# One PSUM bank moved from C's rows of a state-space scan to a third accumulator of the experts and attention

## The chip, the cores and the metric

The kernel runs on one core of one Trainium2 chip. The metric is the device time of one launch in microseconds; a verdict compares runs of two kernels on the same chip. Five engines work side by side, each on its own queue in order: TensorE (PE, with its weight loads shown as PEld), VectorE (DVE), ScalarE (ACT), GpSimd (POOL) and SyncE (SP), which issues nearly all DMAs.

## The reference, cut to what matters

Eight rows of x, 512 tokens by 256 channels each, go through two layers. Layer 0: a gate with eight exponential averages, a Mamba block, then a small expert-chosen linear map and a top-2 of 8 expert FFN. Layer 1: a linear pair with low-rank corrections, attention with 8 heads, an adapter with layernorm, and a top-4 of 32 expert FFN with a shared expert. All is float32. The change sits in the Mamba block:

```python
def step(h, inp):                                   # per token t
    x_t, dlt, B_t, C_t = inp                        # 512 channels, 16 states
    dA = jnp.exp(dlt[:, None, :] * A[None])
    h = dA * h + dlt[:, None, :] * B_t[:, :, None] * x_t[:, None, :]
    y_t = jnp.einsum('bn,bnd->bd', C_t, h) + D * x_t
    return (h, y_t)
...
y = ys.transpose(1, 0, 2) * jax.nn.silu(z)
return jnp.einsum('bld,md->blm', y, W_out)          # added to x
```

## The kernel before

The program is written as generators that yield after each piece of work, and a planner interleaves them; a compiler then fixes the order of each engine's queue. `thread_x` makes layer 0's gate and Mamba block, row by row. `thread_y` makes the rest for a group of rows: routing, experts' tiles, then attention. The groups are rows [0], [1, 2], [3, 4, 5], [6, 7]. While `thread_y` works on one group, `thread_x` is advanced so that the share of its cost that is done keeps step with the share of `thread_y`'s (L1170 to L1182). Row 0 of `thread_x` has no partner. The last group of `thread_y` runs beside the routing of layer 1's experts (`top4`), row 7's routing follows alone (L1201), then come 95 expert tiles and the final gather.

In `thread_x` a row has a head and 64 items. The head (`head`, L471 to L707) is cut into some 65 pieces: gate, averages, projections, convolution, and delta and delta times x, which go to DRAM as `packs`. It uses `gx`, a PSUM tag of two banks. Item n = (b, j, g, k) handles a quarter k of channel block j, 32 channels, with four of the 16 states, group g; so 128 partitions hold 32 channels by 4 states. `begin(n)` (L747) starts an item two ahead: ACT's exp gives dA (L752), POOL multiplies delta times x by B's row (L754, tile h, 8 buffers). `run(n)` (L774) lets DVE scan over time (L780) and multiply the result by C's row (L781). Four products later `add` (L785) lets PE sum them over the states into the bank `yp` (L790). `gate` and `finish` (L797, L805) complete the row: y times silu(z) on POOL, W_out on PE, the sum with x, and the store to `xa`.

The rows of B and C over 128 partitions come from a matmul of a 0/1 matrix (`states`) with the row's bf16 pieces. B's row is made once per (b, g), in a `gx` bank, and copied to SBUF by ACT (`get_B4`, L728). C's row is made by PE at k = 0 of every (b, j, g), 128 times in all, straight into a PSUM bank of its own, `c4` (L777 to L779), and DVE reads it there. The bank is single, so the next C matmul waits in PE's queue until the last product has read it. The chains written by `in_order` (L156) keep `thread_x`'s own instructions in program order on each engine.

PSUM has eight banks: gx 2, c4, yp in `thread_x`'s pool; g 2 and acc 2 in `thread_y`'s. `acc` (L870) takes the experts' transposed tokens and outputs, and attention's values, transposes and sums (L1032, L1062, L1078). In `top4`, the shared expert's two output banks are `yp` and `c4` (L1145).

Each item of the main loop also advances the head of a later row by one piece, and by a second at every twelfth (L852 to L854): some 70 pieces in a row's 64 items, so heads move ahead of their row over time.

Of the kernel before, what the change touches and what calls it, by code (L numbers as in the profile page):

```python
# [13 lines left out]
ALU = mybir.AluOpType  # L14
# [37 lines left out]
def adaln_attn_ffn_kernel(ctx: ExitStack, tc: tile.TileContext, d: dict, out: bass.AP):  # L52
# [23 lines left out]
    def mm(o, pairs):  # L76
        for i, (lhsT, rhs) in enumerate(pairs):
            nc.tensor.matmul(o, lhsT, rhs, start=(i == 0), stop=(i == len(pairs) - 1))  # L78
# [317 lines left out]
    def thread_x(wp, wk, ps):  # L396
        def load(name, shape):
            t = wp.tile(shape, F32, tag=name, name=name)
            nc.sync.dma_start(t, d[name])
            return t  # L400

        def gx():
            return ps.tile([P, T], F32, tag="gx", name="gx", bufs=2)
# [15 lines left out]
        W_in = load("W_in", [P, KC, 1024])  # L419
        W_x = load("W_x", [P, 4, 96])  # L420
        W_dt = load("W_dt", [64, 512])
        W_out = load("W_out", [P, 4, C])


        alpha = wp.tile([P, 9], F32, tag="alpha", name="alpha")
# [45 lines left out]
        def head(b):  # L471
# [97 lines left out]
            yield  # L569
            nc.gpsimd.tensor_tensor(soma[:, 1, :], soma[:, 1, :], s1, ALU.mult)  # L570
            yield
            cen = wk.tile([P, KC, T], F32, tag="cen", name="cen")
            sq = wk.tile([P, KC, T], F32, tag="gated", name="sq")
            p0 = project(Wout, soma, 0)
            yield
# [138 lines left out]
        def states(g):  # L714
            return quads[:, g].rearrange("k n c -> k (n c)")

        packs = [dram.tile([4, P, 2, T], F32, name=f"pack{i}", tag=f"pack{i}") for i in range(2)]
        xzs = [dram.tile([P, 4, 2, T], F32, name=f"xzs{i}", tag=f"xzs{i}") for i in range(2)]
        got, B4s = {}, {}

        def get_pack(b, j, k):

# [2 lines left out]
            nc.sync.dma_start(t, src[None].to_broadcast([4, 32, 2, T]))  # L725
            got[b, j, k] = t

        def get_B4(b, g):  # L728

            pt = gx()  # L730
            mm(pt, [(states(g), rows[b])])
            t = wk.tile([P, T], F32, tag="B4", name="B4", bufs=4)
            nc.scalar.copy(t, pt)
            B4s[b, g] = t


        fold = wp.tile([P, 32], F32, tag="fold", name="fold")
# [4 lines left out]
        ready = set()  # L742
        due, product = {}, []
        items = [(b, j, g, k) for b in range(NB) for j in range(4) for g in range(4) for k in range(4)]
        yps, Cs, hs, dAs, xz, y8s = {}, {}, {}, {}, {}, {}

        def begin(n):  # L747

            b, j, g, k = items[n]
            t = got[b, j, k]  # L750
            dA = wk.tile([P, T], F32, tag="dA", name="dA", bufs=4)
            nc.scalar.activation(dA, t[:, 0, :], AF.Exp, scale=A[:, 4 * j + k, g : g + 1])  # L752
            h = wk.tile([P, T], F32, tag="h", name="h", bufs=8)
            nc.gpsimd.tensor_tensor(h, t[:, 1, :], B4s[b, g], ALU.mult)  # L754
            hs[n], dAs[n] = h, dA
            if (g, k) == (1, 3):
                xz[b, j] = wk.tile([P, 2, T], F32, tag="xz", name="xz")
                nc.sync.dma_start(xz[b, j], xzs[b % 2][:, j])
            if j == 0 and g < 3 and k == 1:
                get_B4(b, g + 1)  # L760

            if j < 3 and (g, k) == (2, 3):
                get_pack(b, j + 1, 0)
            if j < 3 and g == 3 and k < 3:
                get_pack(b, j + 1, k + 1)
            if j == 3 and b + 1 < NB and g == 3:
                if k == 0:
                    get_pack(b + 1, 0, 0)
                if k < 3:
                    get_pack(b + 1, 0, k + 1)  # L770
                if k == 3:
                    get_B4(b + 1, 0)

        def run(n):  # L774
            b, j, g, k = items[n]
            h = hs[n]
            if k == 0:  # L777
                Cs[0] = ps.tile([P, T], F32, tag="c4", name="c4")
                mm(Cs[0], [(states(4 + g), rows[b])])  # L779
            nc.vector.tensor_tensor_scan(h, dAs.pop(n), h, 0.0, ALU.mult, ALU.add)  # L780
            product[:] = [nc.vector.tensor_tensor(h, h, Cs[0], ALU.mult).ins]  # L781
            if k == 3:
                due.setdefault(n + 1, []).append(lambda: add(n - 3))

# [12 lines left out]
        def gate(b, j, n):  # L797
# [4 lines left out]
            if j == 3:  # L802
                due.setdefault(n + 2, []).append(lambda: finish(b, 0, n + 2))

        def finish(b, e, n, x=None):  # L805

            if e == 0:
                x = wk.tile([P, KC, T], F32, tag="cen", name="xr")
                nc.sync.dma_start(x, d["x"][b])
            pt = gx()  # L810
            mm(pt, [(W_out[:, j, ts(e, P)], y8s[b][:, j, :]) for j in range(4)])

            def sum_():
                nc.vector.tensor_tensor(x[:, e, :], x[:, e, :], pt, ALU.add)
                if e == 0:
                    finish(b, 1, n + 1, x)
                else:
                    nc.sync.dma_start(xa[b], x)
                    done.add(b)

            due.setdefault(n + 1, []).append(sum_)

        def pieces():

            for b in range(NB):
                for i, _ in enumerate(head(b)):
                    if b == 0 and i == 14:
                        prepare()
                    yield

        H = pieces()
# [2 lines left out]
            yield 3  # L834
        for k in range(4):
            get_pack(0, 0, k)
        get_B4(0, 0)
        begin(0)
        begin(1)
        N = len(items)  # L840
        for n in range(N):
            b, i = divmod(n, 64)
            if i == 58 and b + 1 < NB:
                while b + 1 not in ready:
                    next(H)
                    yield 0
            if n + 2 < N:
                begin(n + 2)
            run(n)
            for f in due.pop(n, ()):  # L850
                f()
            next(H, None)  # L852
            if i % 12 == 4:
                next(H, None)  # L854
            yield 4
        while due:
            n = min(due)
            for f in due.pop(n):
                f()
            yield 4  # L860

    def thread_y(q, bs, ps):
# [5 lines left out]
            return ps.tile([P, T], F32, tag="g", name="g", bufs=2)  # L868

        def acc():  # L870
            return ps.tile([P, T], F32, tag="acc", name="acc", bufs=2)

        with ExitStack() as ph:
            wp = ph.enter_context(tc.tile_pool(name=f"w2_{q}", bufs=1))
# [214 lines left out]
    def top4(wp, wk, ps):  # L1089
# [7 lines left out]
        def ps_tile():  # L1097
            return ps.tile([P, T], F32, tag="gx", name="g4", bufs=2)
# [3 lines left out]
        def route(b):  # L1102
# [39 lines left out]
            yield from dispatch(b, c, ti, dest4, counts, wk, ps_tile, ps_tile, E4, K4, CAP4, tab4, "tab4")  # L1142

            yield 1
            yp = [ps.tile([P, T], F32, tag=t, name="y4p") for t in ("yp", "c4")]  # L1145
            for f in range(KC):
                pa = ps_tile()
                mm(pa, [(sh["Ws1"][:, k, ts(f, P)], c[:, k, :]) for k in range(KC)])
# [212 lines left out]
```

## Time and profile before

| | us |
|---|---|
| median of 3 runs | 4148.91 (4148.35 to 4155.98) |
| the profiled execution | 4169.97 |
| its span | 4168.2 |
| PE busy in it | 3258.9 (78%) |
| DVE busy | 2635.8 (63%) |
| ACT busy | 1799.2 (43%) |
| POOL busy | 1612.5 (39%) |
| mean granted TensorE clock | 0.875 of full speed |

Busy time is an average over stages. Row 0's scans run from 155 to 420 us, rows 1 to 5's from 420 to 2014, rows 6 and 7's to 2832; attention of the last group and the layer 1 routing run to 3740, the expert tiles to 4080, the gather to the end. A group of instructions is told by line, engine, operation, tile written and tiles read, shape and count; then busy time in us and the mean of one in ns; then the idle time of the engine just before them and what ended most of it. A row of the waits gives who waited for whom, us in total, times, and the longest.

### The profile page before, as it was taken

To read this page: it belongs to the slowest core of one execution; us is meant where nothing else is said; L and a number is where in the kernel's file an instruction comes from. 1 tells how busy PE (TensorE), PEld (TensorE's weight loads), DVE (VectorE), ACT (ScalarE), POOL (GpSimd) and SP (SyncE) were. 2 spreads that over 40 slices of the span, in tenths; PEclk is the share of its full clock that TensorE was granted. 3 is DMA by queue.
4 is the path that set the end of the run, shared out by engine and by line. 5 is a ranking of instruction groups with operands and counts; after the bars stand their busy time and mean duration, and the time that the engine had idled before them with its cause. 6 is when DMAs were issued, how large, how long until landed. Compare 5 with 4: busy or idle time off the path is not lost. (4 is left out here: it accounts for less than half of the span.)

```text
span 4168.2 us, 36840 instructions
## 1 busy us (share of the span) xinstructions
PE 3258.9 (78%) x10964; PEld 1653.5 (40%) x10964; DVE 2635.8 (63%) x4178; ACT 1799.2 (43%) x2890; POOL 1612.5 (39%) x1222
## 2 busy tenths in 40 slices
PE   4425586888577788798669698889988999969894
PEld 1101153333254333333337433333466444437772
DVE  4597886798966888888972555764432443433336
ACT  2425465457267367357345333442322343322222
POOL 0445645355536435336353421320043111134552
PEclk7656687998788899799889799999989999989996
DMA  4555676445345312312245312213044112118776
GB/s 107 204 182 205 216 280 217 152 176 206 129 162 163 95 49 84 97 58 74 83 147 187 125 51 72 63 53 100 23 177 146 56 49 75 36 59 260 244 237 223
DMA packets 159372, 554.77 MB, mean 133 GB/s; under 512 B 27731, under 2 KB 34290, under 8 KB 146757
## 3 DMA queue, kind: packets, MB, share of 16 engines
q1 hardware_dynamic: 135076, 501.35, 36.3%
q0 software_dynamic: 24096, 51.08, 3.3%
q8 instruction: 87, 1.43, 0.1%
q14 instruction: 113, 0.92, 0.1%
HBM read 453.00 MB, written 234.82 MB: 165 GB/s over the span
## 5 line engine op out<-in xcount | busy, mean ns | idle before, releaser
L754 POOL TENSOR_TENSOR h<-packed,B 128x512 f32<-128x512 f32 x512 | 813.0, 1610 | 895.4 <-PE yp L790 536.6
L780 DVE TENSOR_TENSOR_SCAN h<-dA,h 128x512 f32<-128x512 f32 x512 | 791.8, 1546 | 77.1 <-POOL h L754 55.6
L752 ACT ACTIVATE dA<-packed,Aexp 128x512 f32<-128x512 f32 x512 | 357.7, 717 | 497.6 <-DVE h L780 346.3
L174 POOL DMA_INDIRECT tok<-ys,to_i x310 | 313.6, 1012 | 456.1 <-DVE ys L959 222.3
L1082 PE MATMUL acc<-aT,V 128*128 128x512 f32 x1024 | 454.3, 598 | 4.1 <-DVE aT L1066 3.9
L781 DVE TENSOR_TENSOR h<-h,c 128x512 f32<-128x512 f32 x512 | 350.1, 684 | 81.5 <-PE c L78 67.5
L174 POOL DMA_INDIRECT tab<-row,si x192 | 198.3, 1033 | 511.3 <-issue 235.4
L1082 PEld LDWEIGHTS acc<-aT,V 128*128 128x128 f32 x1024 | 193.5, 191 | 248.6 <-issue 231.6
L78 PE MATMUL acc<-wv,c 128*128 128x512 f32 x512 | 262.3, 630 | 4.7 <-DVE aT L1066 3.1
L1052 DVE TENSOR_REDUCE nm<-g 128x1 f32<-128x512 f32 x256 | 164.4, 682 | 115.9 <-PE g L1042 114.4
L78 PE MATMUL g<-xT,fw 128*128 128x256 f32 x960 | 231.2, 394 | 7.8 <-ACT h L952 7.8
L78 PE MATMUL acc<-fw,h 128*128 128x256 f32 x960 | 223.1, 386 | 5.2 <-DVE ys L959 5.2
L78 PE MATMUL c<-bc,quads 96*128 96x512 bf16 x128 | 57.8, 451 | 209.0 <-DVE h L781 205.5
L790 PE MATMUL yp<-h,fold 128*32 128x512 f32 x1024 | 217.5, 742 | 0.7 <-DVE h L781 0.7
L1055 ACT ACTIVATE ex<-g,nm 128x512 f32<-128x512 f32 x256 | 173.6, 683 | 102.8 <-DVE nm L1052 98.2
L78 PEld LDWEIGHTS g<-xT,fw 128*128 128x128 f32 x960 | 186.7, 199 | 44.7 <-ACT h L952 9.4
L78 PEld LDWEIGHTS acc<-fw,h 128*128 128x128 f32 x960 | 184.7, 194 | 44.9 <-issue 8.3
L1065 PE MATMUL acc<-ident,ex 128*128 128x128 f32 x1024 | 154.1, 283 | 53.6 <-ACT ex L1057 17.1
L1057 ACT ACTIVATE ex<-ex,den 128x512 f32<-128x512 f32 x256 | 176.6, 720 | 35.3 <-DVE den L1056 34.5
L1086 DVE TENSOR_TENSOR x<-x,acc 128x512 f32<-128x512 f32 x64 | 43.6, 682 | 231.2 <-PE acc L1082 231.2
L1065 PEld LDWEIGHTS acc<-ident,ex 128*128 128x128 f32 x1024 | 118.9, 143 | 176.3 <-issue 51.5
L1042 PE MATMUL g<-qk 64*128 64x512 f32 x512 | 159.8, 671 | 33.2 <-ACT ex L1055 20.6
(284 smaller groups left out, 5720.4 us busy)
## 6 DMA issues: line engine op xcount, KB each, us to landing
fw<-in_fW SPq DMA_DIRECT2D x60, 1154.0 KB
tab<-zeros SPq DMA_DIRECT2D x32, 2112.0 KB
packed<-pack SPq DMA_DIRECT2D x128, 512.0 KB
mw<-in_mW SPq DMA_DIRECT2D x95, 384.0 KB
tab<-zeros SPq DMA_DIRECT2D x16, 2080.0 KB
xt<-tab SPq DMA_DIRECT2D x95, 264.0 KB
pack<-dd SPq DMA_DIRECT2D x32, 512.0 KB
xz<-xzs SPq DMA_DIRECT2D x32, 512.0 KB
```

The lines of the kernel that those rows point to most:

```text
L78: nc.tensor.matmul(o, lhsT, rhs, start=(i == 0), stop=(i == len(pairs) - 1))
L174: i = nc.gpsimd.indirect_dma_start(out=table_, out_offset=bass.IndirectOffsetOnAxis(ap=idx, axis=0), in_=src, in_offset=None, bounds_check ...
L752: nc.scalar.activation(dA, t[:, 0, :], AF.Exp, scale=A[:, 4 * j + k, g : g + 1])
L754: nc.gpsimd.tensor_tensor(h, t[:, 1, :], B4s[b, g], ALU.mult)
L780: nc.vector.tensor_tensor_scan(h, dAs.pop(n), h, 0.0, ALU.mult, ALU.add)
L781: product[:] = [nc.vector.tensor_tensor(h, h, Cs[0], ALU.mult).ins]
L790: chain([nc.tensor.matmul(yps[0][32 * k : 32 * k + 32, :], fold, hs.pop(n + k), start=(g == 0), stop=(g == 3)) for k in range(4)])
L1052: nc.vector.tensor_reduce(nm, sp, AX.X, ALU.max, negate=True)
L1055: read.append(nc.scalar.activation(ex, sp, AF.Exp, bias=nm, accum_out=den).ins)
L1057: nc.scalar.activation(ex, ex, AF.Identity, scale=den)
L1065: nc.tensor.transpose(tp[:, m, :], ex[:, ts(m, P)], ident)
L1082: nc.tensor.matmul(ys[k], V[:, m, C * u + P * k : C * u + P * (k + 1)], aTs[u][:, m, :], start=(u == 0 and m == 0), stop=(u == 1 and m == 3))
```

## The change

C's row is made beside B's, once per (b, g), in `gx` and copied to SBUF by ACT: `get_B4` becomes `get_rows`, and the product reads the copy. The bank `c4` goes; `acc` gets three banks. In `top4` the second output bank of the shared expert is taken from `gx`. The copies of C need 8 KB of each partition of SBUF. Room is made in two ways: W_out no longer stays in SBUF but is loaded per row, with x, into the buffer `xc` (`get_fin`), which the head of a row also uses; and the head's `cen` shares the buffer of `gm`. So that the head of row b + 2 does not take `xc` first, it is held after its first piece until row b + 1's items run.

```diff
-        W_out = load("W_out", [P, 4, C])
...
-            cen = wk.tile([P, KC, T], F32, tag="cen", name="cen")
+            cen = wk.tile([P, KC, T], F32, tag="gm", name="cen")
...
-        def get_B4(b, g):
-
-            pt = gx()
-            mm(pt, [(states(g), rows[b])])
-            t = wk.tile([P, T], F32, tag="B4", name="B4", bufs=4)
-            nc.scalar.copy(t, pt)
-            B4s[b, g] = t
+        def get_rows(b, g):
+
+            for t, u in (("B4", g), ("C4", 4 + g)):
+                pt = gx()
+                mm(pt, [(states(u), rows[b])])
+                q = wk.tile([P, T], F32, tag=t, name=t, bufs=4)
+                nc.scalar.copy(q, pt)
+                four[t, b, g] = q
...
-            nc.gpsimd.tensor_tensor(h, t[:, 1, :], B4s[b, g], ALU.mult)
+            nc.gpsimd.tensor_tensor(h, t[:, 1, :], four["B4", b, g], ALU.mult)
...
-            if k == 0:
-                Cs[0] = ps.tile([P, T], F32, tag="c4", name="c4")
-                mm(Cs[0], [(states(4 + g), rows[b])])
             nc.vector.tensor_tensor_scan(h, dAs.pop(n), h, 0.0, ALU.mult, ALU.add)
-            product[:] = [nc.vector.tensor_tensor(h, h, Cs[0], ALU.mult).ins]
+            product[:] = [nc.vector.tensor_tensor(h, h, four["C4", b, g], ALU.mult).ins]
...
+        fin, at = {}, [0, 0]
+
+        def get_fin(b):
+
+            assert at[0] <= b + 1 or at[1] < 8
+            fin[b] = wk.tile([P, 4, T], F32, tag="xc", name="fin")
+            nc.sync.dma_start(fin[b][:, 0:2, :].rearrange("p k (a c) -> p (k a) c", a=2), d["W_out"])
+            nc.sync.dma_start(fin[b][:, 2:4, :], d["x"][b])
+
         def finish(b, e, n, x=None):
 
             if e == 0:
-                x = wk.tile([P, KC, T], F32, tag="cen", name="xr")
-                nc.sync.dma_start(x, d["x"][b])
+                x = fin[b][:, 2:4, :]
             pt = gx()
-            mm(pt, [(W_out[:, j, ts(e, P)], y8s[b][:, j, :]) for j in range(4)])
+            w = fin[b][:, 0:2, :].rearrange("p k (a c) -> p (k a) c", a=2)
+            mm(pt, [(w[:, j, ts(e, P)], y8s[b][:, j, :]) for j in range(4)])
...
+            if b > 0 and i == 3:
+                get_fin(b - 1)
             if n + 2 < N:
                 begin(n + 2)
             run(n)
             for f in due.pop(n, ()):
                 f()
-            next(H, None)
-            if i % 12 == 4:
-                next(H, None)
+            for _ in range(1 + (i % 12 == 4)):
+                if at[0] <= b + 1:
+                    next(H, None)
             yield 4
+        get_fin(NB - 1)
...
-            return ps.tile([P, T], F32, tag="acc", name="acc", bufs=2)
+            return ps.tile([P, T], F32, tag="acc", name="acc", bufs=3)
...
-            yp = [ps.tile([P, T], F32, tag=t, name="y4p") for t in ("yp", "c4")]
+            yp = [ps.tile([P, T], F32, tag="yp", name="y4p"), ps_tile()]
```

More of the change, by code (lines that the diff above doesn't have):

```diff
@@ L718, in thread_x @@
         xzs = [dram.tile([P, 4, 2, T], F32, name=f"xzs{i}", tag=f"xzs{i}") for i in range(2)]
-        got, B4s = {}, {}
+        got, four = {}, {}
         def get_pack(b, j, k):
@@ L744, in thread_x @@
         items = [(b, j, g, k) for b in range(NB) for j in range(4) for g in range(4) for k in range(4)]
-        yps, Cs, hs, dAs, xz, y8s = {}, {}, {}, {}, {}, {}
+        yps, hs, dAs, xz, y8s = {}, {}, {}, {}, {}
         def begin(n):
@@ L759, in begin @@
             if j == 0 and g < 3 and k == 1:
-                get_B4(b, g + 1)
+                get_rows(b, g + 1)
             if j < 3 and (g, k) == (2, 3):
@@ L771, in begin @@
                 if k == 3:
-                    get_B4(b + 1, 0)
+                    get_rows(b + 1, 0)
         def run(n):
@@ L828, in pieces @@
                         prepare()
+                    at[:] = [b, i]
                     yield
@@ L836, in thread_x @@
             get_pack(0, 0, k)
-        get_B4(0, 0)
+        get_rows(0, 0)
         begin(0)
```

## The prediction

> **What bounds it now.** I read the page's busy table first, then engine busy by stretch, then the groups and waits of the tiles that the change touches, last the two timelines that decide. The stretches are cut at the first and last scan of each row of the state-space stage (64 scans a row):
>
> ```profile
> 155.00:420.00 265.00, 107.80 (x247) 28.28 (x248) 225.37 (x206) 119.87 (x154) 160.10 (x94) 0.61 0.54 191
> 420.00:717.00 297.00, 203.55 (x723) 112.14 (x722) 241.06 (x302) 168.04 (x229) 172.97 (x119) 0.78 0.66 235
> ...
> 1705.00:2014.00 309.00, 270.14 (x779) 106.54 (x780) 274.35 (x331) 175.46 (x274) 141.44 (x86) 0.92 0.23 73
> ...
> 2424.00:2832.00 408.00, 364.81 (x1128) 149.37 (x1127) 249.35 (x371) 164.19 (x321) 109.92 (x68) 0.96 0.19 59
> ```
>
> After the stretch and its length come PE, PEld, DVE, ACT, POOL busy, then clock and DMA. Row 0 (155 to 420) has no partner: DVE is busy 225 of 265 us, PE 108. Rows 1 to 5 (420 to 2014) run beside attention and experts: DVE 1310 of 1594 us (82%), PE 1252 (79%), so each waits for the other. In row 7 PE is busy 89% and DVE 61%; from 2832 to 3740 PE is over 90%. So DVE sets the pace in row 0, DVE and PE together in rows 1 to 5, PE later.
>
> ```profile
> L754 POOL TENSOR_TENSOR h<-packed,B 128x512 f32<-128x512 f32 x512 | 813.0, 1610 | 895.4 <-PE yp L790 536.6
> L780 DVE TENSOR_TENSOR_SCAN h<-dA,h 128x512 f32<-128x512 f32 x512 | 791.8, 1546 | 77.1 <-POOL h L754 55.6
> ...
> L781 DVE TENSOR_TENSOR h<-h,c 128x512 f32<-128x512 f32 x512 | 350.1, 684 | 81.5 <-PE c L78 67.5
> ...
> L78 PE MATMUL c<-bc,quads 96*128 96x512 bf16 x128 | 57.8, 451 | 209.0 <-DVE h L781 205.5
> ```
>
> The c bank is single: TensorE stands 205.5 us in its queue until DVE's product has left the bank, and DVE waits 67.5 us for the new c. By the waits of each stretch, PE's are 84.6 us in row 0, 97.9 in rows 1 to 5, 23.1 later; DVE's are 0, 54.7, 12.8.
>
> **A price that the rows hide.** The scan averages 1546 ns, but its minimum is 1184 and its median 1219; the product is 656 to 690 ns always. The DVE timeline, then POOL's, of row 0:
>
> ```profile
> 319.78 0.69 DVE L781 TENSOR_TENSOR h<-h,c 128x512 f32<-128x512 f32 x1
> 320.38 1.44 DVE L780 TENSOR_TENSOR_SCAN h<-dA,h 128x512 f32<-128x512 f32 x1
> 321.86 0.69 DVE L781 TENSOR_TENSOR h<-h,c 128x512 f32<-128x512 f32 x1
> 322.46 1.50 DVE L780 TENSOR_TENSOR_SCAN h<-dA,h 128x512 f32<-128x512 f32 x1
> ```
>
> ```profile
> 320.70 12.99 POOL L754 TENSOR_TENSOR h<-packed,B 128x512 f32<-128x512 f32 x6
> ```
>
> POOL runs six multiplies back to back at 2.16 us each (1.26 alone), DVE one scan and one product in 2.1 us: lockstep. Laying the timelines over each other, a scan that meets no POOL multiply takes 1215 ns (234 of them), one that meets one 1825 (278). The product takes 684 ns in both cases (274 and 238). Scan has both tensors in SBUF; product has one in PSUM. The same split holds for the other DVE operations with two SBUF tensors: L547 750 alone, 1270 met; L601 749 and 1533; L658 694 and 1484. After the change the product has two SBUF tensors.
>
> **The rules.** The Trainium skill, "SBUF — State Buffer", section "SBUF: two separate sides", says that DVE and GpSimd share a port pair as an exclusive lock, taken by a DVE operation with two SBUF inputs against a GpSimd one that reads SBUF; the second blocks until the first is done. That speaks against this change. Taken literally, the 204 products that start inside a POOL multiply's last 1267 ns would wait 183 us together. The trace is milder: scan plus POOL operation in lockstep need 2.16 us, not 1.215 + 1.267 = 2.48, so a POOL multiply holds the pair about 0.92 us. With that window the overlap of products with POOL is 24 us in row 0, 73 in rows 1 to 5, 24 in rows 6 and 7, together 121; with the full 1267 ns it is 28, 92 and 30, together 150. I use the overlap, not the wait, since what exceeds the product is already waited for by the next scan. The page "VectorE: DVE Perf Modes", section "Rules for kernel authors", on the other hand advises copying matmul output to SBUF when many operations read it. By it the 16 products per copy ought to be cheaper; by the trace they are not: L242, f32 128x512 from SBUF, takes about 0.69 us, the product from PSUM 0.684. I take zero gain from that and the 121 to 150 us of lock as cost.
>
> **Part by part.** *C from SBUF.* Removed: 128 c matmuls x 451 ns = 58 us of PE. Added: 32 gx matmuls x 446 ns = 14 us, and 32 copies x 576 ns (row of B's copy) = 18 us of ACT, which is 43% busy; the compiled order also has 6 more ACT table loads x 1283 ns = 8 us. ACT's work hides beside DVE; with no cover, those 26 us would be the price. C's matmul and copy join B's at two gx banks: PE waits 12.6 us for a B copy in rows 1 to 5 and 21 in row 0 now. Doubling that costs 0 to 15 us of PE, nothing in row 0; I take 3.
>
> *Row 0:* products gain 24 to 28 us of lock and lose no wait of theirs (DVE's c wait is 0). PE's 84.6 us there were free. With the product, lock demand is 129 us of two-SBUF DVE work + 94 POOL multiplies x 0.92 + 44 of product = 259 of 265 us, so little of it can hide: +26.
>
> *Rows 1 to 5:* +80 us of lock on DVE, the middle of 73 and 92. Gone are DVE's 54.7 us for c. PE loses 97.9 us of waiting and 60 matmuls x 451 = 27 us of work. DVE operations that now wait for PE there (x for acc 25.3, ys 23.4, wi 12.4, nm, aT, V, some 85 us in all) come earlier; I credit a fifth to a third of it, 20 us, because the experts' and scores' chains stay. Late next is DVE itself, with lock waits. 80 - 55 - 20 = +5, between -45 (lock falls into idle time) and +45 (no relief).
>
> *Rows 6 and 7:* DVE is 61% busy, so 24 to 30 us of lock hide. PE loses 23.1 us of waits and 24 x 451 = 11 us of work, about half on the path: -15 (0 to -34).
>
> *Third accumulator.* What a free bank can end is small: PE's waits before acc for an eviction are 15.6 us (L1065 for V), 5.2 (experts for ys), 4.6 (values for aT), 25 in all, next to nothing of it after 2832, where PE is full. -2 (0 to -15).
>
> *y4p's second bank from gx.* One of two gx banks is held while both branches of the shared expert pass through the other, so pb's matmul waits for the silu of pa (597 ns). 14 such turns x about 0.8 us = 11 us if nothing stands between; the compiled order puts attention matmuls between most: +3 (0 to 11). In the last row the scatters hide it: the schedule is written at 3737.7, the fence falls at 3747.0.
>
> *W_out and x per row, in xc's buffer.* Seven more loads of 512 KB, 3.7 MB of 555. SP's queue gets 7 more issues of 0.33 us at about the place of x's load. Now the first output matmul waits for the load too, and behind it in PE's queue stand yp's folds and the head. In rows 1 to 5 x was issued 28 to 54 us ahead of that matmul, in row 0 only 4.8 (425.9 against 430.7), so row 0 may pay 0 to 5: +1. The load waits for POOL's last read of xc, which the order has before it: 0. Heads no longer run ahead of their row: in the order the head falls behind by up to 30 DVE instructions, but row 0 to 1 has no lead today and no gap (420.2, 420.1): 0 to 10, taken as 0. cen in gm's buffer: gm's last reader is long done, 0.
>
> **Sum.** 26 + 5 + 3 - 15 - 2 + 3 + 1 = +21 us. The profiled execution took 4169.97 us (span 4168.2 and 1.8 around it), 0.5% above the 4148.91 median of the timed runs; the difference is put on the median: 4149 + 21 = 4170 us.
>
> **Rivals.** *Faster: decoupling wins.* The lock's waits fall where DVE idles (284 us in rows 1 to 5) and the in-order stall behind c was what made both engines idle. Then rows 1 to 5 give -55 - 25 with lock half hidden (+35) = -45, row 0 +20, rows 6 and 7 -25, banks -5: 4094 us or so. For it: two engines at 80% with neither full. Against: DVE is at 89% in row 5, where c is only 6 us of its idle time. It decides from the point where less than half of the lock lands on DVE's path.
>
> *Slower by more: POOL starves.* If POOL gets the pair only after scan and product, h arrives late and DVE waits (already 35.8 us in row 0). One further product per item on row 0's and rows 1 to 5's path is 384 x 0.684 = 263 us at worst, of which a quarter is +65: 4149 + 21 + 65 = 4235.
>
> *It does nothing that can be told:* gains and lock cancel within 8 us; 4149.
>
> **Chances.** About 0.2% (8 us) is what a measurement can tell from no change. Slower by more than that 0.57 (0.45 moderate, 0.12 starving), same 0.14, faster 0.29. The likeliest case's own range is 4158 to 4200. The 8-in-10 range drops the outer part of both rivals: 4080 to 4235.
>
> **What would show it.** Product mean up from 684 to about 0.9 us, with a split by POOL overlap like the scan's; no PE wait for DVE's product; DVE busier by 100 us or more over rows 0 to 5; row 0 longer by 20 to 30 us; acc waits barely changed. I am wrong if the product stays at 684 (no lock), or if rows 1 to 5 shorten by more than 30 us (PE's stall was the coupling), or if rows lengthen through late heads, seen as DVE waits for packed or xc.

## The result, and the profile after

The changed kernel takes 4281.22 us (median of 4 runs, 4279.51 to 4288.08) beside 4151.03 us for the kernel before on the same chip: ratio 1.0315, interval 1.0297 to 1.0333. It is 130 us slower; the prediction was 21 us slower, at most 86. The profiled execution took 4288.08 us with a span of 4286.0, so 118 us more than the profiled one before.

The stretches, cut at the first scan and last product of the rows as before: rows 0, 1, 5, then 6, 7 and all that follows. After stretch and length come PE, PEld, DVE, ACT, POOL busy, the granted clock and the DMA share.

```profile
156.00:443.00 287.00, 144.94 (x244) 31.20 (x244) 258.43 (x206) 122.44 (x157) 160.59 (x96) 0.62 0.50 179
443.00:760.00 317.00, 226.21 (x704) 114.27 (x704) 261.21 (x302) 167.75 (x230) 166.40 (x118) 0.77 0.62 220
1765.00:2101.00 336.00, 274.52 (x757) 107.00 (x757) 287.26 (x327) 181.87 (x283) 134.17 (x84) 0.87 0.21 69
2101.00:2591.00 490.00, 394.95 (x1354) 221.20 (x1353) 308.83 (x474) 211.58 (x334) 195.80 (x149) 0.86 0.37 120
2620.00:2941.00 321.00, 273.95 (x814) 111.85 (x813) 248.48 (x296) 128.18 (x248) 112.84 (x68) 0.90 0.20 62
2941.00:4286.00 1345.00, 1156.16 (x4359) 686.15 (x4357) 545.49 (x1464) 406.90 (x781) 371.94 (x377) 0.94 0.40 131
```

In row 0 VectorE does the same 206 instructions in 258 us instead of 225, and the row is 22 us longer; row 1 does 302 in 261 instead of 241 and is 20 us longer. Rows 6 and 7 are divided differently (row 6 now holds expert work that row 7 held before), so they are compared together. From the instructions' times in each profile:

| stretch | length before | after | all products together, before | after | VectorE idle, before | after |
|---|---|---|---|---|---|---|
| row 0 | 265 | 287 | 44.0 | 75.5 | 39.6 | 28.6 |
| rows 1 to 5 | 1594 | 1658 | 218.6 | 310.6 | 284.3 | 272.1 |
| rows 6 and 7 | 818 | 840 | 87.5 | 122.1 | 317.9 | 273.9 |
| the rest | 1336 | 1345 | | | 799.1 | 799.5 |

The loss arises where products are: 22 + 64 + 22 + 9 us are nearly the whole 118. The groups of the scan's tile, in the columns of the prediction's fence:

```profile
L754 POOL TENSOR_TENSOR h<-packed,B 128x512 f32<-128x512 f32 x512 | 810.7, 1604 | 870.0 <-PE yp L787 524.3 <-DMA packed<-pack 242.6 <-ACT B L733 71.0
L777 DVE TENSOR_TENSOR_SCAN h<-dA,h 128x512 f32<-128x512 f32 x512 | 809.0, 1580 | 78.0 <-POOL h L754 54.9 <-ACT dA L752 22.3
L778 DVE TENSOR_TENSOR h<-h,C 128x512 f32<-128x512 f32 x512 | 508.2, 993 | 11.5
...
L787 PE MATMUL yp<-h,fold 128*32 128x512 f32 x1024 | 346.3, 718 | 226.4 <-DVE h L778 206.7 <-DVE y L796 14.0 <-DVE si L275 3.0
```

Three things are to be seen. The product went from 684 to 993 ns: 158 us over 512. Laid over POOL's timeline, the products that meet no POOL instruction still take 688 ns (252 of them), those that meet a POOL multiply 1425 (211). VectorE waits for nothing that c caused: 67.5 us before, 0 now. But TensorE still waits for the product: the 205.5 us ahead of c are gone, and 206.7 us ahead of the fold into `yp` (the matmul of `add`, which sums a product over the states) have come. Before, the fold stood behind c's wait, and its products were done when its turn came:

```profile
L790 PE MATMUL yp<-h,fold 128*32 128x512 f32 x1024 | 217.5, 742 | 0.7 <-DVE h L781 0.7
```

Now its weight loads wait for the product as well, 317.9 us. And VectorE has a new wait, for the output matmul ahead of the sum with x (`fin`). The rows of the waits after:

```profile
PEld yp L787 <- DVE h L778: 317.9, 103, 12.2
...
PE yp L787 <- DVE h L778: 206.7, 84, 12.1
...
DVE fin L820 <- PE gx L78: 56.4, 13, 12.4
```

How the product is held up is seen in row 0. VectorE's timeline, then POOL's, of the kernel after:

```profile
333.05 2.28 DVE L777 TENSOR_TENSOR_SCAN h<-dA,h 128x512 f32<-128x512 f32 x1
335.36 1.57 DVE L778 TENSOR_TENSOR h<-h,C 128x512 f32<-128x512 f32 x1
336.85 2.28 DVE L777 TENSOR_TENSOR_SCAN h<-dA,h 128x512 f32<-128x512 f32 x1
339.17 1.58 DVE L778 TENSOR_TENSOR h<-h,C 128x512 f32<-128x512 f32 x1
```

```profile
336.34 11.49 POOL L754 TENSOR_TENSOR h<-packed,B 128x512 f32<-128x512 f32 x6
```

Before, one POOL multiply (2.16 us) passed per item of VectorE (2.1 us). Now an item takes 3.80 us (333.05 to 336.85) and POOL makes two multiplies in it (1.92 us each): the two engines take turns, one instruction each. A scan takes 1.06 us more than its 1.22 alone, a product 0.88 more than its 0.69. POOL does not lose by it; VectorE pays once per instruction that has two SBUF tensors, and now there are two such instructions in an item.

### The profile page after: what moved, and what is told of

The parts are those of the page before. It is cut to its first block, busy times and chain, and to the rows that moved or that the text cites. A ratio compares the mean times of both kernels' runs of the same rounds, so it can differ in the third digit from the quotient of the medians.

```text
span 4286.0 us, 36510 instructions
## 1 busy us (share of the span) xinstructions
PE 3367.6 (79%) x10868; PEld 1666.2 (39%) x10868; DVE 2819.6 (66%) x4183; ACT 1817.6 (42%) x2923; POOL 1623.3 (38%) x1222
## 5 line engine op out<-in xcount | busy, mean ns | idle before, releaser
L754 POOL TENSOR_TENSOR h<-packed,B 128x512 f32<-128x512 f32 x512 | 810.7, 1604 | 870.0 <-PE yp L787 524.3
L777 DVE TENSOR_TENSOR_SCAN h<-dA,h 128x512 f32<-128x512 f32 x512 | 809.0, 1580 | 78.0 <-POOL h L754 54.9
L787 PE MATMUL yp<-h,fold 128*32 128x512 f32 x1024 | 346.3, 718 | 226.4 <-DVE h L778 206.7
L778 DVE TENSOR_TENSOR h<-h,C 128x512 f32<-128x512 f32 x512 | 508.2, 993 | 11.5
L787 PEld LDWEIGHTS yp<-h,fold 128*32 128x32 f32 x1024 | 41.4, 116 | 445.6 <-DVE h L778 317.9
L331 DVE SCALAR_TENSOR_TENSOR to_m<-xt,sc_teb 128x8 f32<-128x8 f32 (+1 forms) x155 | 44.5, 287 | 239.9 <-DMA xt<-tab 239.8
L78 PE MATMUL g<-xT,mw 128*128 128x256 f32 x760 | 182.5, 384 | 0.0
```

The costliest lines, as they stand in the source:

```text
L754: nc.gpsimd.tensor_tensor(h, t[:, 1, :], four["B4", b, g], ALU.mult)
L778: product[:] = [nc.vector.tensor_tensor(h, h, four["C4", b, g], ALU.mult).ins]
L787: chain([nc.tensor.matmul(yps[0][32 * k : 32 * k + 32, :], fold, hs.pop(n + k), start=(g == 0), stop=(g == 3)) for k in range(4)])
```

## The experiments

The theory after the result: the lock (the turns that a VectorE instruction with two SBUF tensors takes with POOL) alone makes the loss; removing c's waits was worth nothing, because TensorE's waits for the product only move to the fold. Its rivals: the folds, which now trickle in and keep TensorE from other work; the room made in SBUF (late heads, loads of W_out); the bank y4p took from gx; or an order of the queues that happened to be worse. All ratios are to the kernel before on the same chip.

Each edit also lets the compiler order the queues anew, so that work can move from beside the rows to behind row 7. Total times compare well only where this order stays. The number of matmuls behind row 7's last product tells: 4315 before, 4357 after. Where it is far from that, a run is also read up to the last product of row 5, to which nearly the same matmuls belong.

**The lock without the rest of the change.** In the kernel before, the product reads B's row in SBUF in place of c, so C is left out of the computation.

```diff
-            product[:] = [nc.vector.tensor_tensor(h, h, Cs[0], ALU.mult).ins]
+            product[:] = [nc.vector.tensor_tensor(h, h, B4s[b, g], ALU.mult).ins]
```

> The kernel before, with one edit: the product's second operand is B's row in SBUF in place of C's row in PSUM (leaves C out of the output). W_out, x, cen, the heads, the c bank, its 128 matmuls and the two accumulators stay as before. Theory 1 (the shared port pair): the product goes from 684 to about 990 ns, and the time to 4230 to 4280 us, most of the +130 of the change, although c no longer makes TensorE or VectorE wait. Theory 2 (the room made in SBUF: W_out and x loaded per row, heads held back): 4130 to 4155 us, since none of that is here. Theory 3 (the third accumulator and the new order of the queues): also 4130 to 4155.

Measured: 4316.06 us, ratio 1.0348 (1.0326 to 1.0369); that is over the range named, on a chip where the kernel before takes 4173.92 us. The product takes 996 ns. One operand of one instruction gives the whole loss; but c's wait is gone here too, so the trickling folds are not yet excluded (TensorE waits 198.9 us ahead of `yp`). The order changed much as well: 4669 matmuls follow row 7. Up to row 5 this run is 95 us longer than before.

**The room without the rest.** The kernel before, with W_out and x loaded per row into `xc`, `cen` in `gm`'s buffer and the heads held back; C stays in PSUM.

> The kernel before, with only the room made: W_out and x loaded per row into the buffer xc, cen in gm's buffer, the head held after its first piece. C stays in its PSUM bank, two accumulators. Theory 1 (port pair): 4145 to 4170 us, at most the waits for the output sum that the changed kernel's trace shows (42 us on VectorE in rows 1 to 5, of which part is on the path). Theory 2 (room): 4230 us or more. Theory 3 (accumulator): 4145 to 4160.

Measured: 4158.21 us, ratio 0.9958 (0.9939 to 0.9978). The room costs nothing, though VectorE's wait for the sum with x is here too (47.3 us). This version is 0.4% faster than the kernel before; VectorE's wait for c fell to 35.3 us in it. I did not find out whether that comes from the room or from the new order of the queues.

**The lock with c's waits kept.** As the first run, with a dependency that lets the c matmul wait for the last product, as it did when the product read the bank. C is left out.

```diff
-                mm(Cs[0], [(states(4 + g), rows[b])])
+                i = nc.tensor.matmul(Cs[0], states(4 + g), rows[b], start=True, stop=True)
+                if product:
+                    tc.add_manual_dep(i.ins, product[0].name, SYNC)
```

> The kernel before with the product's second operand in SBUF (B's row; leaves C out), as in the first experiment, but the c matmul is made to wait for the last product, as it does in the kernel before. So the four folds into yp again stand behind a wait that covers all their products, and only the port pair is new. Theory 1 (port pair alone): the time equals that of the first experiment within 20 us, ratio to before 1.030 to 1.037. Theory 4 (new, from the traces: without the c wait each fold waits for its own product at the head of TensorE's queue, and TensorE loses some 130 us of side-by-side folds): ratio 1.012 to 1.025, folds' busy time back from 346 to about 218 us.

Measured: 4310.75 us, ratio 1.0354 (1.0310 to 1.0398). Its groups:

```profile
L783 DVE TENSOR_TENSOR h<-h,B 128x512 f32<-128x512 f32 x512 | 502.5, 981 | 11.8
...
L792 PE MATMUL yp<-h,fold 128*32 128x512 f32 x1024 | 215.0, 733 | 4.9 <-DVE h L783 4.9
L779 PE MATMUL c<-bc,quads 96*128 96x512 bf16 x128 | 58.4, 456 | 266.7 <-DVE h L783 266.6
```

The fold is back to what it was (4.9 us of waits, busy 215.0 us) and TensorE waits 266.7 us for c, yet the time is that of the first run, 1.0354 against 1.0348. Since the orders differ, here are the stretches from row 0's first scan to row 5's last product, then those behind row 7; in each of the two sets the kernel before, the first run, this run:

```profile
155.00:2014.00 1859.00, 1359.70 (x4227) 601.28 (x4228) 1535.08 (x1851) 1013.40 (x1475) 936.25 (x610) 0.83 0.43 149
153.00:2108.00 1955.00, 1466.02 (x4228) 615.20 (x4229) 1675.62 (x1864) 1004.72 (x1460) 952.41 (x611) 0.84 0.41 142
152.00:2105.00 1953.00, 1370.37 (x4234) 605.65 (x4234) 1670.87 (x1862) 1009.92 (x1465) 958.03 (x610) 0.83 0.41 142
...
2832.00:4168.00 1336.00, 1159.61 (x4316) 687.11 (x4314) 536.92 (x1457) 405.96 (x778) 371.85 (x377) 0.93 0.40 130
2852.00:4316.00 1464.00, 1265.68 (x4669) 737.39 (x4667) 582.25 (x1545) 449.28 (x872) 371.47 (x377) 0.93 0.37 123
2956.00:4299.00 1343.00, 1161.20 (x4320) 685.69 (x4320) 539.82 (x1459) 405.40 (x779) 373.28 (x377) 0.93 0.39 130
```

Up to row 5, with nearly the same matmuls, the two runs are alike (1955 and 1953 us against 1859). So it is all the same to the time whether TensorE waits for the product at c, with the folds side by side, or at the folds, which then trickle in. That alone does not say that either wait is free; the next run bears on it. And this run keeps the order of the kernel before nearly to the end (4320 matmuls behind row 7 against 4315): it is the cleanest measure of the lock, 94 us up to row 5, 33 in rows 6 and 7, 7 behind them, in one profile of each.

**Decoupling without the lock.** The kernel before, C still in PSUM, but in one of three gx banks, with the folds one item later, so that no bank of C's own is waited for.

```diff
-                Cs[0] = ps.tile([P, T], F32, tag="c4", name="c4")
+                Cs[0] = gx()
...
-                due.setdefault(n + 1, []).append(lambda: add(n - 3))
+                due.setdefault(n + 2, []).append(lambda: add(n - 3))
```

> The kernel before, with C's row still read from PSUM, but taken from gx, which gets c4's bank and so has three; the folds are put one item later. The product keeps one SBUF operand, and C's next matmul need not wait for the last product when a bank is free. The shared expert's second output is taken from gx too. Theory 1 and 4: product 684 ns, c waits of TensorE and VectorE under half of 205 and 68 us, time 0.5 to 2% below before (ratio 0.98 to 0.995). If the coupling through c cost nothing: 0.995 to 1.005.

Measured: 4181.01 us, ratio 1.0024 (1.0009 to 1.0039). The waits of this run:

```profile
PEld yp L790 <- DVE h L781: 101.1, 39, 13.3
PE yp L790 <- DVE h L781: 60.2, 19, 13.0
PE gx L78 <- DVE h L781: 44.9, 12, 7.4
DVE h L781 <- PE gx L78: 39.2, 16, 5.9
```

TensorE's 205.5 us for c became 44.9 + 60.2, VectorE's 67.5 became 39.2, and the total gained nothing. That is the prediction's first rival, "decoupling wins", tried without the lock. But the order changed here too: 4600 matmuls follow row 7. Up to row 5 the run is 11 us shorter than the kernel before (1848 against 1859), with 12 more matmuls still to do. So the waits are worth little, but not shown to be worth exactly nothing.

**Folds one item later in the kernel after**, so that they wait less for the last product.

> The changed kernel, with the folds into yp put one item later, so that all four products are done when TensorE comes to them (gate is put one item later too). Theory 1: no more than 15 us faster than the changed kernel, ratio to before 1.027 to 1.034. Theory 4: TensorE's 207 us of waits for the product go to under 80 us, folds' busy time from 346 towards 220 us, and the time falls by 30 to 70 us: ratio 1.012 to 1.024.

Measured: 4296.67 us, ratio 1.0304 (1.0265 to 1.0343). TensorE's wait ahead of `yp` fell only from 206.7 to 163.0 us and the folds' busy time from 346 to 298, short of what was expected, and 4578 matmuls follow row 7. The total did not change. Up to row 5 the run is 29 us shorter than the kernel after, with 28 more matmuls still to do, so a small effect of the folds is not excluded.

**The third accumulator taken back**: the kernel after with two `acc` banks, y4p's second bank its own again.

> The changed kernel, but with two accumulators, and the freed bank given to the shared expert's second output alone, as before. Theory 1 and 4: the third accumulator is worth 0 to 20 us, so the ratio to before is 1.030 to 1.038. Theory 3 (third accumulator and its order do the harm): 1.000 to 1.015.

Measured: 4297.36 us, ratio 1.0308 (1.0267 to 1.0349), against 1.0315 with three. The run takes both back at once, so it shows that the third bank and y4p's turn through gx together are worth nothing, not each alone. The order moved here too (4496 matmuls follow row 7), but up to row 5 the two agree, at 1941 and 1945 us.

**POOL's multiply taken away**, in the kernel after and in the kernel before: ACT copies delta times x to h, so that the multiplication by B is left out.

```diff
-            nc.gpsimd.tensor_tensor(h, t[:, 1, :], four["B4", b, g], ALU.mult)
+            nc.scalar.copy(h, t[:, 1, :])
```

> The changed kernel, with GpSimd's multiply by B's row replaced by a ScalarE copy of delta times x (leaves B out of the output), so that GpSimd reads no SBUF beside the scans. To be compared with the same edit on the kernel before. Theory 1 (port pair): scan about 1220 ns, product about 690, and the two edited kernels within 30 us of each other; this one 4020 to 4130. Theory 2 or 3: the pair still stands 100 us or more apart.

> The kernel before, with GpSimd's multiply by B's row replaced by a ScalarE copy (leaves B out of the output): the base for the same edit on the changed kernel. All theories: scan about 1220 ns, VectorE 170 us less busy; the time 4020 to 4130 unless ScalarE, with 300 us more work, becomes the bound in row 0. Theory 1: within 30 us of the edited changed kernel. Theories 2 and 3: 100 us or more below it.

Measured: after 4107.35 us, 0.9845 (0.9826 to 0.9864); before 4037.0, 0.9682 (0.9664 to 0.9700). The product after:

```profile
L778 DVE TENSOR_TENSOR h<-h,C 128x512 f32<-128x512 f32 x512 | 395.9, 773 | 11.3
```

It did not fall to 684, because 65 products still meet the POOL instructions of the heads, at 1353 ns. The difference of the two kernels shrank from 130 to 70 us; the products are now 46 us longer ((773 - 684) x 512) and the scans 12 us. Less lock, less loss, but the pair did not become equal: the result lies between the two theories, which named under 30 and over 100 us. By VectorE's busy time the two differ by 65 us, so nearly all of it is on the path here; they also differ in all else that the change does.

**The lock taken away with C in SBUF.** In the kernel after (two `acc` banks), exp writes dA into the freed bank, and the scan works in it; scan and product then have one SBUF tensor each. dA has a single bank, so ACT's exp waits for the product.

```diff
-            nc.vector.tensor_tensor_scan(h, dAs.pop(n), h, 0.0, ALU.mult, ALU.add)
-            product[:] = [nc.vector.tensor_tensor(h, h, four["C4", b, g], ALU.mult).ins]
+            dA = ps.tile([P, T], F32, tag="c4", name="dA")
+            nc.scalar.activation(dA, got[b, j, k][:, 0, :], AF.Exp, scale=A[:, 4 * j + k, g : g + 1])
+            nc.vector.tensor_tensor_scan(dA, dA, h, 0.0, ALU.mult, ALU.add)
+            product[:] = [nc.vector.tensor_tensor(h, dA, four["C4", b, g], ALU.mult).ins]
```

> The changed kernel with two accumulators, the freed bank now holding dA: ScalarE's exp writes it there, the scan runs in place in the bank, the product reads scan and C's copy and writes h. So scan and product have one SBUF tensor each. The bank is single, so exp, scan and product of one item follow each other; the exp comes at the scan and not two items ahead; packed has six buffers, since dA's left SBUF. The shared expert's second output uses the bank later, as c4 before. Theory 1: scan 1220 ns and product 690 ns with no split by GpSimd's multiplies, VectorE 150 to 170 us less busy than before; if its other work fills the gaps behind the exp the ratio to before is 0.965 to 0.985, if it waits 0.3 us per item for the exp 0.99 to 1.01. Rival (no port pair involved): the scan stays at 1.5 us, ratio 1.03 or more.

Measured: 4153.07 us, ratio 1.0011 (0.9998 to 1.0025). Its groups:

```profile
L752 POOL TENSOR_TENSOR h<-packed,B 128x512 f32<-128x512 f32 x512 | 672.2, 1335 | 946.9 <-PE yp L787 424.4 <-DMA packed<-pack 344.3 <-ACT B L733 51.0
L777 DVE TENSOR_TENSOR_SCAN dA<-dA,h 128x512 f32<-128x512 f32 x512 | 627.6, 1226 | 360.0 <-ACT dA L776 319.8 <-POOL h L752 35.9 <-POOL dd L666 2.8
...
L778 DVE TENSOR_TENSOR h<-dA,C 128x512 f32<-128x512 f32 x512 | 352.1, 688 | 13.9
```

The same C in SBUF, and product, scan and POOL's multiply all at their lone times (688, 1226, 1335 ns): the whole 3% comes back, though VectorE now waits 319.8 us for the exp. The scan's lock, which the kernel before pays too, is gone as well and helps (VectorE is busy 2466.9 us against 2635.8), so this is not the product's lock alone. With a second bank for dA this might beat the kernel before; there was no bank left for it, and it was not tried.

**Is it only VectorE's time?** If so, any work of that size on VectorE must cost as much. To the kernel before, an unused maximum over 232 columns of C's bank is added behind each product, from PSUM alone; then over 400 columns; then a reciprocal of 40 columns, as a delay that the compiler's order might not count.

```diff
             product[:] = [nc.vector.tensor_tensor(h, h, Cs[0], ALU.mult).ins]
+            nc.vector.tensor_reduce(idle, Cs[0][:, 0:232], AX.X, ALU.max)
```

> The kernel before with one more VectorE operation behind each of the 512 products: a maximum over 232 columns of the c bank, one input and that in PSUM, about 0.3 us, so that VectorE gets as much more work per item as the changed kernel gives it (product 684 to 993 ns), with no further use of the shared port pair. Its result is not used. Theory 1 (VectorE's time itself is what the kernel pays for, though VectorE is busy only 82% in rows 0 to 7): ratio to before 1.025 to 1.04, like the changed kernel. Rival (the harm comes through GpSimd, whose multiplies get the pair later and hold up the scans, and VectorE's idle time would take up 0.3 us per item): 1.000 to 1.015.

> The kernel before with a longer idle VectorE operation behind each product: a maximum over 400 columns of C's bank, from PSUM alone, its result unused. From 390 ns for 232 columns and 680 ns for 512 in the profile of the run with 232, about 565 ns each, 289 us in all; less what the scans gained and other rows lost there, VectorE should be busy some 180 us longer than before, as in the run whose product reads two SBUF tensors and whose C waits (183 us). Theory 'VectorE time only, the first 100 us fit into gaps': ratio to before 1.025 to 1.04. Theory 'the lock costs by its bursts with GpSimd, not by VectorE's time': 1.002 to 1.012, since 232 columns cost 1.003.

> The kernel before with a reciprocal of 40 columns of C's bank behind each product, its result unused. A reciprocal of 512 columns took 3352 ns in the profile of before, so about 0.3 to 0.4 us each by the clock, some 180 us in all, as the 232-column maximum, but of few columns, so that whatever fixes the order of the queues may hold it for short, as it does with the lock's delay. Theory 'a delay that the order does not know of is what costs': 1.02 or more. Theory 'size and place of VectorE's time decide, known or not': 1.000 to 1.006, as with the maximum over 232 columns (1.0027).

Measured: 232 columns 4158.88 us, 1.0027 (1.0015 to 1.0039), in the rival's range; 400 columns 4227.29, 1.0129 (1.0092 to 1.0167), just above the range of the second theory; reciprocal 4164.77, 0.9990 (0.9979 to 1.0002), against the theory of a delay that is not planned for. But the compiled order had changed with the added instruction: 4315 matmuls follow row 7's last product in the profile before, 4237, 4226 and 4238 in these. The part after row 7 is 35 to 48 us shorter, so some price may be hidden. Three more runs have the same number of instructions in each item: 4 columns, in the kernel before and in the one with the lock and c's waits (C left out there), and 232 columns in the latter.

> The kernel before with a maximum over only 4 columns of C's bank behind each product, from PSUM, its result unused. By the line through 390 ns at 232 columns and 566 at 400 it takes about 150 ns, 77 us in all. It has the same number of instructions as the runs with 232 and 400 columns, so it shows what the changed order of the queues alone is worth. If the order gave those runs a gain that hid the price of VectorE's time, this one is faster than before, 0.985 to 0.998. If the gaps of VectorE took the first 100 us, it is 0.999 to 1.003.

> The same 4 columns behind each product in the kernel whose product reads two SBUF tensors and whose C waits for the last product. If the lock has its price whatever the order of the queues, this is 1.03 to 1.04 of before and some 3.3% over the run with 4 columns of the kernel before. If the lock's 1.035 was in good part the luck of an order, the two lie within 1.5 to 2.5%.

> The product on two SBUF tensors, C's wait kept, and the maximum over 232 columns behind each product. If VectorE's time costs little until its gaps are full and then nearly 1 for 1, 100 us more on top of the lock's 180 cost 60 to 100 us: ratio 1.050 to 1.060. If the maximum costs little wherever it stands, and the lock's price is its own, the two add: 1.035 to 1.042.

Measured: 4 columns 4141.63 us, 0.9997 (0.9985 to 1.0008); with the lock 4255.17, 1.0275 (1.0254 to 1.0296), so 2.8% over the run with 4 columns alone, between the two expectations; with the lock and 232 columns 4288.21, 1.0356 (1.0334 to 1.0378), which is the case in which the two add.

The product with the lock and 232 columns behind it, in the last of these:

```profile
L784 DVE TENSOR_TENSOR h<-h,B 128x512 f32<-128x512 f32 x512 | 502.8, 982 | 11.4
L785 DVE TENSOR_REDUCE idle<-c 128x1 f32<-128x232 f32 x512 | 198.8, 388 | 57.1 <-PE c L780 57.1
```

| added behind the product | VectorE busy, no lock | ratio | VectorE busy, lock | ratio | lock's price |
|---|---|---|---|---|---|
| nothing | 2635.8 | 1 | 2815.2 | 1.0354 | 3.5% for 179 us |
| 4 columns | 2653.0 | 0.9997 | 2846.3 | 1.0275 | 2.8% for 193 us |
| 232 columns | 2737.8 | 1.0027 | 2920.4 | 1.0356 | 3.3% for 183 us |
| 400 columns | 2856.5 | 1.0129 | | | |

The lock costs 2.8 to 3.5% in three orders of the queues, so it is not an order's luck; the order can be worth some 0.7% of it. At some 4150 us those are 115 to 147 us for 179 to 193 us of VectorE time: 0.6 to 0.8 us each. By the totals, VectorE time from PSUM is far cheaper: from 4 to 232 columns 0.3% or 12 us for 85, from 4 to 400 columns 1.3% or 55 us for 204; with the lock, from 4 to 232 columns, 0.8% or 34 us for 74.

But in these totals the order has its part: with 4 columns 4270 matmuls follow row 7, with 232 columns 4237, with 4 columns and the lock 4320. Up to row 5 the matmuls are nearly the same, and there one profile of each, with chips of other speed scaled by their kernel before, gives:

| up to row 5 | longer, us | VectorE busier, us | us of run for each |
|---|---|---|---|
| lock, beside nothing added | 94 | 136 | 0.7 |
| lock, beside 4 columns | 96 | 155 | 0.6 |
| lock, beside 232 columns | 106 | 148 | 0.7 |
| 4 to 232 columns, no lock | 20 | 54 | 0.4 |
| 4 to 400 columns, no lock | 58 | 144 | 0.4 |
| 4 to 232 columns, with the lock | 31 | 46 | 0.7 |

These differences are uncertain by some 10 us. At the same dose the lock still costs more (94 to 106 us against 58), but the gap is smaller than the totals make it. With the lock in, the maximum costs as much per microsecond as the lock itself; that fits gaps that are already filled, but no run shows which gaps.

**Does the place in the item make it?** The lock delays the product's end, the maximum behind it does not. So the 400 columns go ahead of the product, in the kernel before.

> The maximum over 400 columns of C's bank, from PSUM, 566 ns each, now ahead of the product instead of behind it, in the kernel before; its result unused. VectorE is given the same extra time as in the run with 400 columns behind the product (1.0129), but now each product, and so the sum that waits for it and the buffer that the sum frees for GpSimd, is late, as with the lock. Theory 'the lock's time costs more because it lies ahead of the product's end': ratio 1.025 to 1.04. Theory 'the place in the item is nothing; the lock's time costs more for another reason, such as its coming in bursts': 1.010 to 1.018.

Measured: 4215.56 us, ratio 1.0077 (1.0047 to 1.0108), VectorE busy 2762.5 us. That is even below the range of the second theory: being ahead of the product does not make the time cost more. The groups show where part of the maximum's time went:

```profile
L781 DVE TENSOR_TENSOR_SCAN h<-dA,h 128x512 f32<-128x512 f32 x512 | 742.3, 1450 | 55.2 <-POOL h L755 48.1 <-ACT dA L753 6.9
...
L782 DVE TENSOR_REDUCE idle<-c 128x1 f32<-128x400 f32 x512 | 282.0, 551 | 69.7 <-PE c L78 69.5
```

The 512 maxima are 282 us of work, but VectorE is only 127 us longer busy; 49 of the missing 155 us are scans that fell from 1546 to 1450 ns. It fits that, while VectorE reads PSUM alone, POOL gets a multiply through without a turn. But at 400 columns behind the product the scans were at 1553, so this is not shown to be the whole reason. Why a microsecond of VectorE's time costs more by the lock (0.6 to 0.7 us up to row 5) than by the maximum (about 0.4) stays open; that it comes in bursts, while POOL fills its eight h buffers, was not tried.

## Why the prediction was wrong, step by step

**Right.** The mechanism: the product meets the lock, splits by POOL's overlap as the scan did, and its mean rose to 993 ns (about 0.9 was named). Row 0: +26 forecast, +22 measured, in part by luck: the lock was 32 us there, more than the 24 to 28 of the forecast, and VectorE's idle time took 11 of it (39.6 to 28.6), where next to nothing was to hide. The third accumulator (-2 forecast), the bank for y4p (+3), the row's copies, the loads (+1): together close to nothing, as the run with two accumulators (1.0308 against 1.0315) and the one with the room alone (0.9958) show; none of these sizes was measured alone.

**Too small: the lock.** The overlap gave 121 to 150 us, by a POOL multiply that holds the pair for 0.92 or for its full 1.267 us, and I took the middle, 26 in row 0 and 80 in rows 1 to 5. (2.16 - 1.215 is 0.945 and not 0.92; the 121 us belong to 0.945, 0.92 gives 117. Little hangs on it.) Measured are 158 us: 32 in row 0 (24 to 28 forecast), 92 in rows 1 to 5 (the upper end of 73 to 92), 35 in rows 6 and 7 (24 to 30). The trace of before had the lockstep, one two-SBUF instruction against one POOL multiply; that a second such instruction takes a second turn in each item follows from it. Then the sum is products met times a turn: 211 x (1425 - 689) = 155 us, with figures that only the profile after has. The wait of 183 us that the prediction worked out from the Trainium skill, "SBUF — State Buffer", section "SBUF: two separate sides", and set aside, is 25 us above the 158 measured, the middle that I took, 136, is 22 us below: neither reading was exact. The trace bears the page out in that one engine blocks the other, but not for a whole instruction: four whole turns would make an item 1.22 + 0.69 + 2 x 1.26 = 4.43 us, and it takes 3.80.

**The step that failed: "80 - 55 - 20 = +5" in rows 1 to 5.** They became 64 us longer. The lock was 92 us, and of the 75 us of credit only 28 can be found: VectorE's idle time fell by 12 us (284.3 to 272.1), and it had some 16 us less other work in these rows. VectorE's 54.7 us for c did go, but others took their place, above all 42.4 us for the output sum:

```profile
DVE fin L820 <- PE gx L78: 42.4, 9, 12.4
```

That wait comes with the room, where it costs nothing (0.9958). TensorE's relief was nil: it waited 97.9 us for the product ahead of c, and now waits 106.0 ahead of `yp`. With c's waits kept and the lock in, rows 0 to 5 take as long as without them (1953 and 1955 us), and decoupling without the lock shortens them by some 11 us, where 75 were credited. I had written "no PE wait for DVE's product" as a sign to look for; 206.7 us of it stand in the profile. What I should have asked is which instruction in its queue needs the product next: the fold, a few entries later.

**The step "rows 6 and 7 -15"** failed in the same way: 24 to 30 us of lock were to hide because VectorE is 61% busy there. The two rows are 22 us longer. In the kernel after, more than the lock changed there: VectorE is busy 66 us longer, 35 of them by the products, and its idle time took 44. The lock with c's waits kept, in the order of before, shows it cleaner: the products take 33 us more, the two rows are 33 us longer, and the idle time fell by only 7 (318 to 311). So the lock did not hide, though VectorE idles over a third of that time; why not stays open.

**The rivals.** "Decoupling wins" (4094) fell with its mechanism. "POOL starves" (4235) was nearest in time but not in cause: VectorE's wait for h is 54.9 us against 55.6, and POOL's multiplies take 810.7 us against 813.0. It is VectorE that loses its turns. Of the some 97 us by which the forecast missed the profiles' difference of 118, rows 1 to 5 make 59 and rows 6 and 7 make 37. In place of +21 the runs put: lock alone +115 to +147 us, everything else within about 20 of nothing.

## What to carry to other kernels

Before a second tensor of a VectorE instruction moves from PSUM to SBUF, look for POOL work beside it: if one two-SBUF instruction is already stretched there, each further one pays a turn of its own, here 0.7 us on 211 of 512 products. Count a wait as removed only after naming the next instruction in the same queue that needs the same producer; here 205.5 us ahead of c became 206.7 us ahead of the fold. And before two versions are compared by their totals, compare the orders of their queues, and cut the profiles where the orders still agree: an added instruction moved some 80 of 4315 matmuls and up to 48 us, another operand moved 354 and 129 us, from one side of row 7's end to the other.

## What the runs showed of the hardware that was not expected

The turns are strict: with POOL busy, scan and product took 2.28 and 1.57 us again and again, for 1.22 and 0.69 alone, and in that lockstep POOL's multiplies became quicker (1.92 us against 2.16), since two pass per item; over the whole run they did not (1604 ns against 1610). POOL's DMA-issuing instructions do not take part: a product that met only these took 696 ns, a scan 1213. And 512 reductions of 232 columns from PSUM, 200 us of work, added 102 us to VectorE's busy time and 11 us to the run; by the stretch up to row 5 their price is higher, about 0.4 us for each microsecond of VectorE, and part of the rest is the order of the queues.
